# Two-layer decoder: moving the second group's cross-attention values and the next mapped keys from layer 1's token loop to the end of the experts

## The chip, the cores and the metric

The kernel runs on one core of one Trainium2 chip. The metric is device time in microseconds (us) of one execution; the median of several runs is compared. Engines are named as in the profile: PE is TensorE (PEld its weight loads), DVE is VectorE, ACT is ScalarE, POOL is GpSimd, and SP's queue issues most DMAs.

## The reference

Sixteen sequences of 256 tokens with 256 features go through two pre-norm decoder layers. Each layer adds three blocks to x. Layer 0: causal linear attention, cross-attention to a context of 77 rows for each sequence, and a mixture of 16 experts (top 2, limited capacity). Layer 1: self-attention with a low-rank latent for keys and values, cross-attention to the same context, and a quantized gated feed-forward block. What matters here is layer 1's cross-attention:

```python
def _L1_xattn_ref(Q, K, V, Wq, bq, Wk, bk, Wv, bv, Wo, bo, mask):   # K = V = ctx_1024
    q = Q @ Wq + bq
    k = K @ Wk + bk
    v = V @ Wv + bv
    scores = jnp.einsum('bqd,bkd->bqk', q, k) * scale
    scores = jnp.where(mask == 0, jnp.asarray(-1000000000.0, scores.dtype), scores)
    probs = jax.nn.softmax(scores, axis=-1)
    attn = jnp.einsum('bqk,bkd->bqd', probs, v)
    return attn @ Wo + bo
```

Neither k nor v depends on x: they can be formed whenever the context and the weights are there.

## The kernel before

**Tiling.** The 4096 tokens are 32 tiles of 128 rows, held on the chip as `E.xs[i]`; a group is four tiles, that is two sequences, so there are `NG = 8` groups. All arithmetic is in 32-bit floats.

**Stages.** `l0_attention` and `l0_cross` are layer 0's attentions; `l0_experts` goes over the 16 experts and writes their rows to device memory (`moe_y`); `l1_tokens` does everything of layer 1 up to the feed-forward block; `l1_ffn` is that block. `l0_experts` and `l1_tokens` are planned separately, but one program follows the other without a barrier, so work of `l1_tokens` that needs no expert starts on PE as soon as the last expert's products (`ps_y`, `ex_y`) are through.

**How `l1_tokens` begins.** Each token's row is x plus two expert rows. `l0_gather` fetches them with two indirect DMAs for a tile (`ex_yg`, issued on POOL, six buffers), `l0_add` adds them on DVE. `front_by_sequence(0)` does this for two tiles at a time: gathers, adds, `layernorm` (statistics and h on DVE, the two steps `ln_rstd` on POOL between them), transposes (`ps_ht`, `hT`), and the projections to the latent and the queries (`ps_pr`). `scores(0)`, the second half, and `front_by_sequence(1)` come next.

**The loop.** For each group g the loop runs over its four tiles: `weighted(i)` finishes tile i's self-attention (`ps_pt` transposes, `ps_av`, `ps_po`), `scores(i + 1)` begins the next one's (`ps_sc`, maxima `sa_top` on DVE, exponentials on ACT, `sa_e` scaled on POOL). Generators are stepped in between: `front(g + 2)`, `combine(g + 2)` (gathers and adds), `cross(g - 1)` (cross-attention of the group before) and `vals`, the values of the group after.

**Keys and values of the cross-attention.** The query, key and output weights are folded beforehand (`X.wqk`, `X.wb`, `X.wvo`). `keys_of(b0)` makes the mapped keys of four sequences, that is two groups: two tiles `ps_k` and one `ps_kb` on PE, each evacuated by ACT to `cx_k0`, `cx_k1` and `cx_kb`. `values(g)` makes what one group needs: `ps_v` on PE (one tile, four products), `cx_v` on DVE, and `cx_bias` in two steps on POOL. Before an even group, `values` first calls `keys_of`. All these tiles have two buffers. Group 0's are recorded ahead of the loop; the others' in the last tile of each turn of the loop.

**What sets the order.** The code above only records operations. `Plan.issue` then simulates the engines with fixed costs and puts the operations in order of their planned begin; on the chip each engine takes its operations in that order. A rank decides among those that could begin within 150 ns of the earliest on an engine: the number of the operation in the recording, plus 60 for those recorded under `urgent(-60)`, the lowest first. A buffer ring adds two rules (`slot_time`): a tile begins only once the tile recorded before it in its ring has begun, and only when the buffer's old user is done. The ring `pp` holds nearly all of PE's outputs in four PSUM buffers, so their order is that of the recording:

```python
    if tile.prior and not tile.prior.started and tile.prior.name not in op.tiles:
        return None
    if tile.older is not None:
        if tile.older.users:
            return None
```

All planned instructions are issued from one helper, so the profile gives L363 for nearly every row; the tiles' names tell them apart.

## Time and profile before

| what | value |
|---|---|
| median of 3 runs | 1718.7 us (1716.73 to 1720.42) |
| profiled execution, its own time | 1710.65 us |
| its span, first to last instruction | 1708.9 us |
| mean granted TensorE clock | 0.963 |
| PE / DVE / ACT / POOL busy | 92% / 65% / 45% / 27% |
| last expert's products (`ps_y`) end | 912.6 us |
| first gather for layer 1 issued | 915.67 us |
| first transpose of layer 1 (`ps_ht`) | 926.58 us |
| last gather issued | 1065.3 us |

Times in a row of the timeline are: start from the beginning of the span, duration, engine, line, operation, output<-inputs, shape, count, and in brackets the engine's idle time before it and what ended it. A busy PE is not PE at its peak. The granted clock is the share of full speed that the throttle allows TensorE.

### The profile page before, as it was taken

Reading aid. Unit: us, or ns where it says so; the run is one execution under the profiler, and the core shown is the slowest. Engines: PE = TensorE matmul, PEld = TensorE weight load, DVE = VectorE, ACT = ScalarE, POOL = GpSimd, SP = SyncE. Lnnn points to the kernel's source line nnn. Section 1 sums busy time; section 2 is a strip of 40 time slices with the busy share of each in tenths; the row PEclk is TensorE's granted clock in tenths of the full one; section 3 lists DMA queues with packets and bytes.
Section 4 is the critical chain, followed back from the end, with each engine's and each line's share of the span. In section 5 each row is a group of like instructions: output and inputs, shape, how many; then the busy total and the mean of one; then the engine's idle time right before and its main releaser. Section 6 shows DMA issues by size and latency. Waiting matters only on the chain.

```text
span 1708.9 us, 24351 instructions
## 1 busy us (share of the span) xinstructions
PE 1564.8 (92%) x9076; PEld 1040.7 (61%) x9076; DVE 1117.3 (65%) x2214; ACT 763.5 (45%) x1965; POOL 458.1 (27%) x538
## 2 busy tenths in 40 slices
PE   6999997998996799999997999999999699999799
PEld 3666664665664577777775665666666444433387
DVE  7988885999996343211223779866767543899951
ACT  4333324667765211211112555555555353667850
POOL 5332112355455200000004787433343200000000
PEclk9999998999997699999998999999999899999899
DMA  6000005611111153433331121000000000001111
GB/s 188 1 1 1 2 3 148 188 47 37 33 40 41 60 163 129 134 131 122 113 99 56 44 65 50 1 1 1 0 1 1 1 1 0 25 25 62 38 49 49
DMA packets 95783, 92.01 MB, mean 54 GB/s; under 512 B 32486, under 2 KB 85438, under 8 KB 95666
## 3 DMA queue, kind: packets, MB, share of 16 engines
q1 hardware_dynamic: 89522, 73.91, 13.8%
q0 software_dynamic: 6144, 16.57, 3.1%
q8 instruction: 71, 1.16, 0.3%
q14 instruction: 46, 0.38, 0.1%
HBM read 52.70 MB, written 36.70 MB: 52 GB/s over the span
## 4 chain that ended last, share of the span: by engine, by line
PE 55%; DVE 27%; issue 7%; ACT 5%; POOL 2%; DMA 2%; SPq 1%; POOLq 0%; DVEq 0%; ACTq 0%
PE ps_y L363 7%; PE ps_h L363 7%; PE ps_pr L363 6%; PE ps_av L363 5%; PE ps_gate L486 5%; PE ps_out L486 5%; PE ps_sc L363 4%; PE ps_pt L363 3%; PE ps_v L363 2%; DVE x L363 2%; DVE sa_top L363 2%; PE ps_po L363 2%; DVE lx_mx L363 2%; DVE lx_s L363 2%; DVE ff_g L1995 2%
## 5 line engine op out<-in xcount | busy, mean ns | idle before, releaser
L363 DVE COPY ex_y<-ps_y 128x256 f32<-128x256 f32 x80 | 33.6, 423 | 217.1 <-PE ps_y L363 217.1
L363 POOL DMA_INDIRECT ex_yg<-moe_y,slot x64 | 63.1, 986 | 344.0 <-DMA moe_y<-ex_y 326.8
L486 PE MATMUL ps_up<-ff_x,ffn_up 128*128 128x512 f32 x336 | 147.0, 595 | 7.1 <-DVE ff_pu L1866 4.3
L363 POOL TENSOR_TENSOR sa_e<-sa_e,sa_rec 128x1024 f32<-128x1024 f32 x64 | 121.4, 1905 | 118.8 <-PE ps_pt L363 64.2
L363 ACT ACTIVATE sa_e<-ps_sc,sa_top 128x256 f32<-128x256 f32 x256 | 118.0, 484 | 74.6 <-DVE sa_top L363 72.3
L363 PE MATMUL ps_h<-ex_xT,w 128*128 128x320 f32 x512 | 144.6, 440 | 0.5 <-ACT ex_h L363 0.5
L363 PE MATMUL ps_y<-w,ex_h 128*128 128x256 f32 x640 | 141.0, 379 | 1.6 <-DVE ex_y L363 1.6
L363 PEld LDWEIGHTS ps_y<-w,ex_h 128*128 128x128 f32 x640 | 121.6, 190 | 20.1 <-DVE ex_y L363 2.0
L363 ACT ACTIVATE ex_h<-ps_h 128x640 f32<-128x640 f32 x64 | 44.9, 703 | 186.6 <-PE ps_h L363 186.6
L363 PEld LDWEIGHTS ps_h<-ex_xT,w 128*128 128x128 f32 x512 | 97.2, 193 | 40.9 <-issue 1.8
L486 PEld LDWEIGHTS ps_up<-ff_x,ffn_up 128*128 128x128 f32 x336 | 63.0, 190 | 91.0 <-issue 73.2
L486 PE MATMUL ps_out<-ffn_down,ff_g 128*128 128x256 f32 x384 | 84.9, 385 | 11.6 <-issue 11.6
L363 ACT ACTIVATE lx_s<-lx_s,lx_mx 128x77 f32<-128x77 f32 x256 | 87.9, 346 | 16.3 <-DVE lx_mx L363 15.9
L486 PE MATMUL ps_gate<-ff_x,ffn_gate 128*128 128x512 f32 x192 | 85.3, 608 | 6.4 <-DVE ff_x L1968 6.4
L486 PEld LDWEIGHTS ps_out<-ffn_down,ff_g 128*128 128x128 f32 x384 | 74.2, 194 | 22.7 <-issue 12.4
L363 DVE TENSOR_REDUCE sa_top<-ps_sc 128x4 f32<-128x1024 f32 x64 | 76.3, 1214 | 14.9 <-PE ps_sc L363 14.6
L363 DVE TENSOR_TENSOR la_at<-ps_sc,la_tri 128x1024 f32<-128x1024 f32 x64 | 75.8, 1213 | 8.6 <-PE ps_sc L363 8.6
L363 POOL DMA_INDIRECT moe_x<-rh,slot x64 | 64.0, 999 | 43.7 <-issue 12.4
L363 PE MATMUL ps_sc<-sa_latT,sa_q 64*128 64x256 f32 x512 | 69.1, 396 | 2.8 <-ACT sa_e L363 2.8
L363 PE MATMUL ps_pt<-ident,sa_e 128*128 128x128 f32 x512 | 65.2, 277 | 6.1 <-ACT ff_x L363 1.9
L486 PEld LDWEIGHTS ps_gate<-ff_x,ffn_gate 128*128 128x128 f32 x192 | 37.4, 195 | 53.9 <-issue 53.1
L363 PEld LDWEIGHTS ps_pt<-ident,sa_e 128*128 128x128 f32 x512 | 57.7, 142 | 15.1 <-issue 3.2
(297 smaller groups left out, 3429.5 us busy)
## 6 DMA issues: line engine op xcount, KB each, us to landing
w<-in_L_ffn_w SPq DMA_DIRECT2D x32, 512.0 KB
moe_x<-rt_zero SPq DMA_DIRECT2D x16, 640.0 KB
ex_xg<-moe_x SPq DMA_DIRECT2D x15, 640.0 KB
moe_y<-ex_y SPq DMA_DIRECT2D x15, 640.0 KB
x<-in_x SPq DMA_DIRECT2D x32, 128.0 KB
out_x<-x SPq DMA_DIRECT2D x32, 128.0 KB
ff_u<-ff_c SPq DMA_DIRECT2D x6, 512.0 KB
ff_c<-ff_u SPq DMA_DIRECT2D x6, 512.0 KB
```

What stands on the lines that cost most here:

```text
L363: made = getattr(getattr(self.nc, self.engine), self.method)(*self.args, **self.kwargs)
L486: E.nc.tensor.matmul(ps, a, b, start=n == 0, stop=n == last)
L1995: nc.vector.scalar_tensor_tensor(gp, low16(gq, I16), sg16, low16(sig, U16), ALU.mult, ALU.mult)
```

## The change

Three things change, all in `l1_tokens`. The mapped keys are kept in a dictionary by pair of groups, so that two pairs can be held. Ahead of the first group's front, under the same `urgent(-60)`, the program now also records the second group's values and the mapped keys of the third and fourth groups. And the loop's first turn forms no values; `values(2)` in the second turn finds its keys made, and from then on the loop is as it was. The operations, their sizes and the numbers of buffers stay the same.

```diff
-        keys = SimpleNamespace()
+        keys = {}
 
         def keys_of(b0):
 
             cols = slice(b0 * S2, b0 * S2 + GK)
-            keys.mapped = []
+            mapped = []
 ...
-                keys.mapped.append(t)
+                mapped.append(t)
 ...
-            keys.term = t
+            keys[b0 // 4] = mapped, t
 
         def values(g):
 
-            if g % 2 == 0:
+            if g // 2 not in keys:
                 keys_of(2 * g)
                 yield
+            mapped, term = keys[g // 2]
             b0 = 2 * (g % 2)
-            C = SimpleNamespace(kT=[t[:, b0 * S2 : (b0 + 2) * S2] for t in keys.mapped])
+            C = SimpleNamespace(kT=[t[:, b0 * S2 : (b0 + 2) * S2] for t in mapped])
 ...
-                bias, keys.term[:, b0 : b0 + 2, :].unsqueeze(2).to_broadcast([P, 2, 2, S2]),
+                bias, term[:, b0 : b0 + 2, :].unsqueeze(2).to_broadcast([P, 2, 2, S2]),
 ...
         with nc.urgent(-60):
+
             step(values(0), 2)
+            step(values(1))
+            keys_of(4)
         f = front_by_sequence(0)
 ...
-            vals = values(g + 1) if g + 1 < NG else none
+            vals = values(g + 1) if 0 < g < NG - 1 else none
```

## The prediction

> **What bounds the kernel now.** I read the page first, for the engines and the chain; then the stretches, cut at the places where the moved work stands; then the timeline round the end of the experts; last the chain through the first turns of the token loop.

> ```profile
> PE 1564.8 (92%) x9076; PEld 1040.7 (61%) x9076; DVE 1117.3 (65%) x2214; ACT 763.5 (45%) x1965; POOL 458.1 (27%) x538
> ...
> PE 55%; DVE 27%; issue 7%; ACT 5%; POOL 2%; DMA 2%; SPq 1%; POOLq 0%; DVEq 0%; ACTq 0%
> ```

> TensorE is the bound over the span, but VectorE holds 27% of the chain, so a TensorE microsecond is worth a microsecond only in some stages. The stretches (columns: length, then busy time and count of PE, PEld, DVE, ACT, POOL; granted clock; DMA) say which:

> ```profile
> core 0: us, PE busy (x) PEld busy (x) DVE busy (x) ACT busy (x) POOL busy (x), PEclk, DMA share, GB/s
> ...
> 918.20:926.58 8.38, 0.00 (x0) 0.03 (x1) 5.83 (x12) 0.00 (x0) 6.07 (x8) 0.64 0.28 78
> 926.58:930.84 4.26, 4.01 (x11) 3.06 (x12) 2.55 (x6) 0.74 (x2) 3.72 (x4) 0.50 0.22 64
> ...
> 957.00:986.60 29.60, 28.57 (x157) 19.69 (x158) 22.08 (x43) 20.26 (x68) 24.05 (x22) 0.94 0.20 58
> 986.60:1043.80 57.20, 53.02 (x298) 34.81 (x297) 48.95 (x101) 29.21 (x98) 44.25 (x39) 1.00 0.19 56
> ...
> 1090.50:1146.70 56.20, 55.15 (x315) 36.42 (x314) 43.54 (x94) 31.98 (x112) 22.44 (x17) 1.00 0.00 1
> ...
> 1017.00:1067.00 50.00, 46.77 (x259) 30.61 (x257) 45.31 (x93) 25.21 (x87) 37.70 (x36) 1.00 0.20 57
> ```

> From 918.20 to 926.58 PE does nothing and ACT does nothing: everybody waits for the first gathered rows. From 1090 on PE is 98% busy. Between them, where the gathers still run on POOL, PE has some slack (53.02 of 57.20) and DVE is nearly full (45.31 of 50, 91%).

> ```profile
> 916.31 1.89 PE L363 MATMUL ps_v<-cx_wvo,w_ctx_T 128*77 128x256 f32 x8
> ...
> 919.52 0.95 POOL L363 DMA_INDIRECT ex_yg<-moe_y,slot  x1 [0.31 <-issue]
> ...
> 922.32 1.80 DVE L363 SCALAR_TENSOR_TENSOR x<-ex_yg,wgt,x 128x256 f32<-128x256 f32 x1 [0.31 <-DMA ex_yg<-moe_y,slot]
> 923.00 0.83 POOL L363 TENSOR_TENSOR cx_bias<-cx_kb,cx_on 128x308 f32<-128x308 f32 x1
> ...
> 924.88 0.34 POOL L363 TENSOR_TENSOR ln_rstd<-ln_mv,eps 128x2 f32<-128x2 f32 x1 [1.05 <-DVE ln_mv L363]
> ...
> 926.58 1.09 PE L363 MATMUL ps_ht<-ident,h 128*128 128x128 f32 x4 [8.38 <-issue]
> ...
> 986.82 1.89 PE L363 MATMUL ps_v<-cx_wvo,w_ctx_T 128*77 128x256 f32 x8
> ...
> 1042.48 1.53 PE L363 MATMUL ps_pt<-ident,sa_e 128*128 128x128 f32 x12 [1.09 <-ACT cx_k L363]
> ```

> This is the path to the first transpose: gather 4, its add, the statistics, two POOL steps (ln_rstd), h, transpose. The second group's values stand at 986.82; the mapped keys of groups three and four end at 1038, and their evacuation on ACT holds PE up at 1042.48.

> ```profile
> 982.14 2.95 DMA ex_yg<-moe_y,slot
> ...
> 999.28 1.53 PE ps_pt L363 x12
> ...
> 1020.83 2.35 DVE sa_top L363 x2
> ```

> The chain is not on PE where the moved work stands: from 974 to 999 it runs through POOL, gathers and DVE adds, and from 1020.8 through DVE.

> **The change part by part.**

> *Removed from the loop, PE.* values(1): 8 matmuls, 1.73 us in the chain's row at 916.47. keys_of(4): 8 matmuls ps_k, 2.34 us, and 4 ps_kb, 1.04 us. Together 5.11 us, the most that the loop can give.

> *Added before the first group, PE.* The same 5.11 us, started at 918.20: values to 919.93, ps_k to 922.27, ps_kb to 923.31. The tiles of this PSUM ring are taken in the order of the program, four buffers: the fourth new tile, ps_kb, needs the buffer of the first ps_v, which cx_v frees at 921.62, before its turn. The first transpose needs the buffer of the second ps_v, freed by the second cx_v on DVE, which stands ahead of h on the same engine. So it fits, 3 us ahead of 926.58. Cost nothing; the cover is the wait for gathers, and without it the 5.11 us would be paid back whole.

> *ACT.* Three evacuations of 0.52 to 0.57 us go into a time in which ACT is idle until 927.49: nothing.

> *DVE.* One cx_v of 0.65 us moves ahead of the fourth add. The fourth gather has landed at 922.3; DVE by then has the third add and cx_v to do. Counted below.

> *POOL.* Two cx_bias steps move from 965 to the front, and more: ranks decide POOL's order. The sixteen new operations ahead of the group's gathers raise the rank of gathers 5 to 8 from 72-75 to 88-91, while the first cx_bias keep 74 and 75 and the new ones have 81 and 82. So all four come right behind gather 4 (ended 920.47), at 0.85 from start to start (965.24 to 966.09), till about 924.0; gather 5 (0.95 and 0.3 of issue) follows, and ln_rstd, waiting for the fourth add, comes behind it at about 925.5 in place of 924.88. Queued behind are gathers 6 to 8. Start of h: 0.6 us later. Bounds: 0, if ln_rstd is planned ahead of gather 5, and +1.9 (0.6 and one more gather of 1.27). I take 0.6. Gathers 6 to 8 come 0.5 to 3 us later; the second half's h was ready at 934.32 and done at 937.44, after the first scores' maxima, which covers that.

> *The adds against POOL.* An add of 0.48 us took 1.80 at 922.32 and ended 0.29 after cx_bias. At 1043.41 six adds beside sa_e and two cx_bias took 1.23, 1.03 and 0.89 for the first three: one add got through between two POOL steps. By that the fourth add ends near 924, as before; that is in the 0.6.

> [...]

> *Clock.* After the empty 8.38 us PE ran at half clock for 4.26 us, with 4.01 busy: 2.0 us lost. The gap left is 3.3 + 0.6 = 3.9 us. The stretch from 957 has a granted clock of 0.94, 3.4 us of half clock, behind an idle time of only 1.75 and 0.35 us at 954.35 to 957.14. So 3.9 us will bring the half clock again: 0, bounds -2.0 (no half clock) and +1.7 (half of another 3.4 us).

> *What the loop makes of the 5.11 us.* From 986.60 to 1043.80 DVE is busy 48.95; without the cx_v of 0.65 it is 48.30. The fullest stretch shown ran DVE at 45.31 / 50 = 0.906; at that rate 48.30 takes 53.3 us, 3.9 less than 57.20. PE would need 47.6 of it. So 3.9 of 5.11 stay and 1.2 go to waits for DVE. Bounds 0 (DVE, POOL and gathers keep their pace) and 5.11; I take 3.9, since the later stretches show that the loop goes at PE's pace when DVE has room. Behind it PE is the bound and hands the gain on to the end. The two adds beside cx_bias at 964.78 and 966.34 took 1.53 and 0.90 in place of 0.47 and 0.45; with cx_bias gone DVE wins 1.5 there, and PE idles 1.03 in that stretch: 0.4 taken, bounds 0 and 1.0.

> Sum: -3.9 - 0.4 + 0.6 + 0 = -3.7 us. The profiled execution took 1710.65 (span 1708.9), so 1706.95 for one like it; the median of the runs is 8.05 higher, 1718.7, and the forecast for it is 1715.0.

> **The rivals.**

> *Nothing comes of it.* The chain says that at 986 and 1035 PE was not what ended last; if the gathers, POOL's sa_e and DVE's order stay the pace to 1066, PE only idles more (0.63 us of wait for DVE at 1066.49 becomes 5 or so). Then -0.4 + 0.6: 1718.9, give or take 2. For it: the chain, POOL's load of 44.25 in 57.20. Against: PE was 53.02 of 57.20 busy, so some of its work did hold the others up, the 1.09 us behind cx_k's evacuation among it.

> *Slower: POOL's order at the front.* If ln_rstd falls behind the four cx_bias and two gathers, h comes 1.9 later, PE's gap grows to 5.2 and one more half-clock window costs 1.7; if then the loop, whose gathers all come 1.6 later up to 965, keeps nothing, the time is 1718.7 + 1.9 + 1.7 = 1722.3. It decides from a first transpose after 928.5. For it: four POOL steps stand where one stood. Against: ln_rstd has a rank of 44 and yields only to what starts before it is ready; POOL's work up to 965 is only 1.64 us more.

> *It all counts.* The moved work fits and the half clock goes too: -5.1 - 1.0 - 2.0 + 0.6 = -7.5, 1711.2. The row at 957 speaks against it.

> **How the numbers follow.** A measurement of this kernel can tell about 0.2%, 3.4 us, from no change. The forecast case (1712 to 1717, chance 0.56, most of it beyond 3.4) and the full gain (0.08) give faster 0.50 and 0.14 to same; nothing (0.20) gives 0.17 to same and 0.03 to slower; POOL's order (0.16) goes to slower but for 0.01. So faster 0.50, same 0.32, slower 0.18. The range goes from the full gain, 1711.2, to the slower case's near side, 1721.8; what it leaves out is about 0.15.

> **What would show it.** Right: no ps_k and no ps_v at the places of 986 and 1035; PE busy about 5 of the 8.4 us behind 918; first transpose at about 927.2; four cx_bias in a row behind the fourth gather; the steps of the later turns (102.8 us for two groups) as before, but earlier by 3 to 4 us. Wrong, if the keys of groups five and six (before at 1144.71) come less than 1 us earlier: then DVE or POOL set the pace; if the first transpose is later than 928.5; or if the planner's order of the loop's first two groups differs so that PE idles more than 10 us between 927 and 1067 (now 11.2, summed from its gaps in the timeline).

## The result, and the profile after

The changed kernel is slower, by a little: its median is 1720.65 us (20 runs, 1717.18 to 1726.34), that of before on the same chip 1717.44 us (20 runs), a ratio of 1.0022 with a 95% interval of [1.0013, 1.0031], or 3.8 us. The forecast was 3.7 us the other way.

Two profiles are compared here by the time behind the end of the last expert product (912.58 us in before, 916.77 in the changed kernel; that difference of 4.19 us lies ahead of the change). The profiled execution of the changed kernel took 1721.74 us, its span 1720.0. The page's engines and chain:

```profile
PE 1573.7 (91%) x9076; PEld 1044.3 (61%) x9076; DVE 1122.2 (65%) x2216; ACT 763.1 (44%) x1963; POOL 459.0 (27%) x538
...
PE 54%; DVE 28%; issue 7%; ACT 5%; POOL 2%; DMA 2%; SPq 1%; POOLq 0%; DVEq 0%; ACTq 0%
```

DVE has two instructions more (2216 for 2214) and ACT two fewer: the planner gave it two more evacuations. The page tells little else, so I go to the front of the layer, in the timeline:

```profile
920.51 3.62 PE L363 MATMUL ps_v<-cx_wvo,w_ctx_T 128*77 128x256 f32 x16
...
923.96 2.24 PE L363 MATMUL ps_k<-w_ctx_T,cx_wqk 128*128 128x308 f32 x8
924.03 1.78 DVE L363 SCALAR_TENSOR_TENSOR x<-ex_yg,wgt,x 128x256 f32<-128x256 f32 x1 [0.86 <-DMA ex_yg<-moe_y,slot]
924.70 0.82 POOL L363 TENSOR_TENSOR cx_bias<-cx_kb,cx_on 128x308 f32<-128x308 f32 x1
...
927.17 1.30 PE L363 MATMUL ps_kb<-w_ctx_T,cx_wb 128*128 128x308 f32 x4 [0.98 <-DVE cx_v L363]
927.25 0.91 POOL L363 TENSOR_TENSOR cx_bias<-cx_bias,cx_drop 128x308 f32<-128x308 f32 x1
...
928.31 1.06 POOL L363 DMA_INDIRECT ex_yg<-moe_y,slot  x1 [0.15 <-issue]
...
929.38 0.20 POOL L363 TENSOR_TENSOR ln_rstd<-ln_mv,eps 128x2 f32<-128x2 f32 x1
...
930.95 0.71 PE L363 MATMUL ps_ht<-ident,h 128*128 128x128 f32 x4 [2.47 <-issue]
```

The front is what the prediction drew: all the moved products before the first transpose, POOL's four `cx_bias` in a row (the first and the last are shown), then a gather, then `ln_rstd`. The first transpose comes 14.17 us behind the last expert product, in before 14.00. Nothing is lost here yet. Next the stretches, from 14.5 us behind the last expert product, cut where tiles 3, 7, 8, 10 and 13 finish their self-attention (the start of the adds `x<-x,ps_po`); columns as before. First the kernel before, then the changed one:

```profile
927.08:998.82 71.74, 64.23 (x355) 45.78 (x353) 54.64 (x104) 43.02 (x142) 56.59 (x51) 0.95 0.18 52
998.82:1050.75 51.93, 48.86 (x263) 31.31 (x264) 45.83 (x97) 25.51 (x87) 39.13 (x36) 1.00 0.18 51
1050.75:1062.15 11.40, 11.40 (x61) 6.87 (x61) 9.03 (x18) 5.88 (x15) 9.61 (x10) 1.00 0.23 65
1062.15:1089.07 26.92, 26.29 (x148) 17.25 (x148) 23.53 (x51) 13.28 (x48) 13.62 (x12) 1.00 0.08 23
1089.07:1125.11 36.04, 35.11 (x208) 22.87 (x206) 25.55 (x49) 20.50 (x71) 13.74 (x10) 1.00 0.00 1
```

```profile
931.27:1003.44 72.17, 63.49 (x347) 45.42 (x346) 53.98 (x104) 43.29 (x142) 55.97 (x49) 0.93 0.18 54
1003.44:1055.14 51.70, 47.98 (x255) 29.79 (x256) 44.83 (x92) 23.08 (x82) 33.98 (x32) 0.97 0.15 44
1055.14:1068.68 13.54, 12.32 (x65) 7.15 (x65) 13.26 (x23) 7.82 (x24) 9.53 (x9) 1.00 0.11 31
1068.68:1100.04 31.36, 28.68 (x154) 18.71 (x153) 25.42 (x53) 11.23 (x40) 18.29 (x17) 0.95 0.14 42
1100.04:1135.96 35.92, 33.47 (x194) 21.51 (x192) 26.14 (x51) 20.43 (x71) 13.74 (x10) 1.00 0.00 1
```

PE's idle time (length less busy) is 12.14 us in before and 18.75 in the changed kernel. Up to tile 3 (71.74 and 72.17 us) and from there to tile 7 (51.93 and 51.70 us) the two need about the same time, though `values(1)` is gone from the first of these stretches and `keys_of(4)` from the second: what left PE didn't shorten them. Then tiles 7 to 10 take 44.90 us for 38.32, with more DVE and POOL work in them than before. From tile 10 on nothing more is lost (the changed kernel is 6.8 us behind at tile 10, 6.7 at tile 13 and 4.8 at tile 31). The chain of waits in the changed kernel's stretch of tiles 8 to 10:

```profile
1071.19 0.95 POOL ex_yg L363
1072.15 0.30 issue
1072.45 2.76 DMA ex_yg<-moe_y,slot
...
1075.30 2.83 DVE x L363
...
1080.16 0.61 DVE sa_aT L363
1080.77 0.04 issue
1080.81 2.62 PE ps_po L363 x8
```

PE stands from 1078.61 to 1080.81 because `sa_aT` is on DVE, behind adds that waited for gathers. In the kernel before, the same view suggests why the moved work was worth so little where it stood (the experiments e7 and e15 test it). `values(1)` stood at 986.82, where the chain runs through POOL, gathers and DVE (974 to 999, shown ahead). `keys_of(4)` stood at 1034.92 to 1038.30, and there the chain is on DVE from 1020.83 until POOL takes it over at 1048.65:

```profile
1026.10 4.13 DVE x L363 x4
...
1034.94 0.18 DVE ln_mv L363
...
1048.65 1.89 POOL sa_e L363
```

In before the last gather is issued 152.70 us behind the last expert product, here 168.06.

### The profile page after: what moved, and what is told of

Its sections match the earlier page's. It is cut to its first block, busy times and chain, and to the rows that moved or that the text cites. A ratio compares the mean times of both kernels' runs of the same rounds, so it can differ in the third digit from the quotient of the medians.

```text
span 1720.0 us, 24344 instructions
## 1 busy us (share of the span) xinstructions
PE 1573.7 (91%) x9076; PEld 1044.3 (61%) x9076; DVE 1122.2 (65%) x2216; ACT 763.1 (44%) x1963; POOL 459.0 (27%) x538
## 4 chain that ended last, share of the span: by engine, by line
PE 54%; DVE 28%; issue 7%; ACT 5%; POOL 2%; DMA 2%; SPq 1%; POOLq 0%; DVEq 0%; ACTq 0%
PE ps_y L363 7%; PE ps_h L363 7%; PE ps_pr L363 6%; PE ps_av L363 5%; PE ps_gate L486 5%; PE ps_out L486 5%; PE ps_sc L363 4%; PE ps_pt L363 3%; DVE x L363 3%; PE ps_v L363 2%; PE ps_po L363 2%; DVE lx_mx L363 2%; DVE sa_top L363 2%; DVE lx_s L363 2%; DVE h L363 2%
## 5 line engine op out<-in xcount | busy, mean ns | idle before, releaser
L363 DVE COPY ex_y<-ps_y 128x256 f32<-128x256 f32 x80 | 33.7, 424 | 217.0 <-PE ps_y L363 217.0
L363 POOL DMA_INDIRECT ex_yg<-moe_y,slot x64 | 63.3, 989 | 348.8 <-DMA moe_y<-ex_y 327.7
L363 ACT ACTIVATE sa_e<-ps_sc,sa_top 128x256 f32<-128x256 f32 x256 | 118.2, 485 | 77.8 <-DVE sa_top L363 75.5
L363 POOL TENSOR_TENSOR sa_e<-sa_e,sa_rec 128x1024 f32<-128x1024 f32 x64 | 121.5, 1906 | 116.8 <-PE ps_pt L363 65.5
L363 PE MATMUL ps_h<-ex_xT,w 128*128 128x320 f32 x512 | 144.6, 440 | 0.5 <-ACT ex_h L363 0.5
L363 PE MATMUL ps_y<-w,ex_h 128*128 128x256 f32 x640 | 141.0, 379 | 1.4 <-DVE ex_y L363 1.4
L363 PEld LDWEIGHTS ps_y<-w,ex_h 128*128 128x128 f32 x640 | 121.5, 190 | 20.0 <-DVE ex_y L363 1.8
L363 ACT ACTIVATE ex_h<-ps_h 128x640 f32<-128x640 f32 x64 | 44.9, 704 | 186.5 <-PE ps_h L363 186.5
L363 PEld LDWEIGHTS ps_h<-ex_xT,w 128*128 128x128 f32 x512 | 97.2, 193 | 40.9 <-issue 1.8
L363 ACT ACTIVATE lx_s<-lx_s,lx_mx 128x77 f32<-128x77 f32 x256 | 87.9, 346 | 16.7 <-DVE lx_mx L363 16.4
L363 DVE TENSOR_REDUCE sa_top<-ps_sc 128x4 f32<-128x1024 f32 x64 | 76.4, 1215 | 19.1 <-PE ps_sc L363 18.8
L363 DVE TENSOR_TENSOR la_at<-ps_sc,la_tri 128x1024 f32<-128x1024 f32 x64 | 75.8, 1215 | 8.6 <-PE ps_sc L363 8.6
L363 POOL DMA_INDIRECT moe_x<-rh,slot x64 | 63.9, 999 | 43.2 <-issue 12.4
L363 PE MATMUL ps_pt<-ident,sa_e 128*128 128x128 f32 x512 | 64.5, 275 | 9.4 <-DVE cx_v L363 4.0
L363 PE MATMUL ps_sc<-sa_latT,sa_q 64*128 64x256 f32 x512 | 70.2, 401 | 0.8 <-ACT sa_e L363 0.8
L363 PE MATMUL ps_po<-sa_wvo,sa_aT 128*128 128x256 f32 x256 | 63.4, 391 | 7.4 <-ACT sa_aT L363 4.4
```

Of the source, the lines that this page charges most:

```text
L363: made = getattr(getattr(self.nc, self.engine), self.method)(*self.args, **self.kwargs)
```

## The experiments

Three theories. **Theory 1**: the first three turns go at the pace of the gathers, POOL and DVE, each working in a fixed order; PE's time is not what ends last, so taking work from it there wins nothing. **Theory 2**: the front costs it, POOL's extra `cx_bias` standing ahead of the gathers. **Theory 3**: the planner, whose costs for DVE and POOL are not the chip's (it counts 0.32 us for an add of gathered rows that took 0.45 to 2.94 in before, and 0.64 for a `cx_bias` step that took 0.75 to 1.00), makes a new order of the early turns, and any new order moves the time. Every ratio is against runs of before on the same chip in the same rounds; on some chips before itself takes 1750 us, most of the difference lying in the stages ahead of this one (e12's span is 24.8 us longer than that of the change's first profile, and its last expert product ends 22.7 us later).

| kernel | ratio to before | tile 13 | last gather | PE idle to tile 13 |
|---|---|---|---|---|
| before (first profile; c1; c3) | 1 | 212.5; 214.3; 214.7 | 152.7; 153.0; 153.9 | 12.1; 11.0; 12.5 |
| the change (first; c2; e12) | 1.0022; 1.0029; 1.0011 | 219.2; 217.9; 220.1 | 168.1; 168.3; 170.5 | 18.8; 20.8; 23.9 |
| e1 values alone | 1.0044 | 225.2 | 161.7 | 21.2 |
| e2 keys alone | 0.9989 | 220.6 | 171.0 | 18.6 |
| e5 front alone | 1.0005 | 215.1 | 156.3 | 12.6 |
| e6 bias late | 1.0014 | 213.9 | 170.9 | 19.0 |
| e7 order kept | 1.0021 | 226.0 | 161.5 | 19.6 |
| e8, e15 fewer products | 1.0000; 1.0005 | 219.0; 212.4 | 156.3; 151.7 | 16.8; 13.4 |
| e11 late gathers | 0.9968 | 216.9 | 169.5 | 13.3 |
| e4 before, gated | 0.9991 | 215.3 | 321.8 | 13.4 |
| change, gated (e3; e10) | 0.9929; 0.9933 | 209.5; 208.1 | 312.5; 311.8 | 12.1; 11.4 |
| e9 bias late, gated | 0.9968 | 204.7 | 314.2 | 9.3 |
| e13, e14 no gathers in the loop | 0.9936; 0.9889 | 207.3; 202.8 | (none) | 7.1; 8.5 |

The last three columns are of one profiled execution each, in us: tile 13 and the last gather by the time behind the last expert product, and PE's idle time from 14.5 us behind it to tile 13. Two profiles of one kernel differ by up to 2.2 us at tile 13 and by about 5 us in the idle time, so the ratios decide.

**Each part by itself (e1, e2).** e1 is the change without the line `keys_of(4)` at the front, e2 the change without `step(values(1))` there, and both do the rest in the loop.

> Only the second group's values go early (1.73 us of PE, one cx_v, two cx_bias); the mapped keys stay in the loop. Theory 1 (the first three turns of the loop, while the gathers run, are paced by DVE and POOL in order; PE work taken out there is not won, and the new order lets the gathers slip behind the turns' own work): the front costs 0.2 us, little PE work is taken out, the gathers end within 3 us of their old place (152.7 us behind the last expert product), and the time is within 2 us of before. Theory 2 (the front: cx_bias ahead of gathers 5 to 8): all of the added POOL and DVE work is here, so the time is like that of the whole change, +3.8 us or so.

Measured: 1.0044 [1.0029, 1.0059].

> Only the mapped keys of groups three and four go early (3.38 us of PE, three ACT evacuations, nothing on DVE or POOL); the second group's values stay in the loop. Theory 1: the gathers slip as in the whole change (they end some 10 to 15 us later than before), and the time is +2 to +5 us. Theory 2 (the front): POOL's front has two cx_bias as before, so the time is that of before or up to 3.4 us less.

Measured: 0.9989 [0.9972, 1.0007]. The smaller part costs 7.7 us and the larger nothing, and together they cost 3.8: the parts don't add up, which speaks for Theory 3, against any sum of parts. Theory 1 as it was put missed both (within 2 us for e1, 2 to 5 us slower for e2), and e1 is also beyond Theory 2's 3.8 us. In both, PE's idle time grew by more than the work that was taken out (to 21.2 us in e1 and 18.6 in e2, from 11 to 12.5).

**The front by itself (e5, e6).** e5 is before, with the same products, evacuations and POOL steps done once more at the front, into buffers that nobody reads:

```diff
+        def spare():
+            ...   # ps_v, cy_v, two cy_bias; two ps_k, ps_kb and their evacuations
         with nc.urgent(-60):
             step(values(0), 2)
+            spare()
```

> The kernel before, and at its front the moved work done once more into buffers that nobody reads (8 + 8 + 4 matmuls, three evacuations, one cx_v, two cx_bias), so that the front is that of the change and the loop's work that of before. Theory 1 (the loss is in the loop's first turns): +0.2 to +2 us. Theory 2 (the front): +3.8 us or more. Theory 3 (any new order of the early turns moves the time by some us, up or down, since the plan's costs for DVE and POOL are not the chip's): anywhere from -5 to +8, with the difference arising behind the third tile and not at the front.

Measured: 1.0005 [0.9993, 1.0016]. The front costs about 0.9 us (at most 2.7), which agrees with its term in the sum (0.6). Theory 2 doesn't explain the 3.8 us.

e6 is the change, but the second group's two `cx_bias` steps wait for the loop's first turn:

```diff
+            if g == 1:
+                yield
             bias = wk.tile([P, 2, 2, S2], F32, name="cx_bias", tag="cx_bias")
```

> The whole change, but the second group's two cx_bias stay in the first turn of the loop; POOL's front then has two cx_bias ahead of gathers 5 to 8 in place of four. Theory 1: the gathers end late as in the change, and the time is that of the change within 2 us. Theory 2 (the front): that of before or less, at least 3 us faster than the change. Theory 3: as likely up as down against the change.

Measured: 1.0014 [1.0001, 1.0027], against 1.0029 [1.0016, 1.0042] for the change in the same rounds (c2); the intervals overlap. Its profile has tile 3 4.4 us earlier than the profile of before on the same chip (c1), but tile 10 only 0.5 us: time won in the first turn is lost by the third. Here are the two controls of these rounds:

> The kernel before once more, for a profile on the chip of the other runs of this set. All theories: its token stage (last expert product to last tile's add, 436.0 us in the first profile) comes out within 3 us of that if the stage repeats itself; if it differs by 5 us or more, single profiles of this stage don't carry differences of a few us.

> The change once more, on the chip of the other runs of this set: 1.002 of before by the first measurement; its gathers end some 15 us later than before's in the same set if that is the order and not the chip.

c1's token stage took 437.7 us, 1.7 more than the first profile's; c2 gave 1.0029. From 14.5 us behind the last expert product to tile 13 c1 took 199.77 us with PE busy 188.75, c2 203.38 with 182.55. So PE had 6.2 us less to do (5.11 moved; c1 also had about 15 us of half clock there, c2 8.5) and idled 9.8 us longer: 3.6 us lost. This is the clearest account of the change.

Half clock doesn't explain the loss: the changed kernel's runs had the higher granted clock (a mean of 0.9635 in c2's 11 runs against 0.9617 in the 27 of before; 0.9580 against 0.9543 in the set of e12). And in the change's three profiles (first, c2, e12) half clock took 17.1, 8.5 and 3.4 us of this stretch, PE was busy 185.9, 182.6 and 181.7 us and idle 18.8, 20.8 and 23.9, and tile 13 came at 219.2, 217.9 and 220.1: PE time that the clock gave back became waiting too.

**What PE's time in the loop is worth (e8, e15).** Both are before with the order of every engine unchanged; only products of `values(1)` and `keys_of(4)` are cut down, while the planner still counts them in full:

```diff
+            E.nc.tensor.matmul(
+                ps[:, :4], a, b[:, :4], start=n == 0, stop=n == last, wide=free(ps))
```

> Before, with every engine's order as it was; only the products of values(1) and keys_of(4) in the loop have 4 columns in place of 256 or 308 (planned at their full cost, evacuated with one column repeated), so 5.11 us of TensorE's time in the loop become about 0.5; nothing is done at the front. Left out: the values of group 1 and the mapped keys of groups 2 and 3. This measures what 4.6 us of TensorE's work at these places are worth by themselves. Theory 1: 0 to 1.5 us, ratio 0.9991 to 1.0000, the idle time of TensorE between tile 3 and tile 10 grows by 3 us or more. Theory 3: 3.5 to 4.6 us, ratio 0.9973 to 0.9980, tile 10 at -3.5 to -4.6.

Measured: 1.0000 [0.9986, 1.0014]. In the trace `ps_v` took 0.65 us for 1.89, and `ps_k` with `ps_kb` 1.50 for 3.38: an instruction with 4 columns still takes time, and about 3.1 us had left PE, not 4.6. The interval allows a gain of 2.4 us, so the ratio says only that they didn't all count. Hence e15, which issues one product for each of the four tiles:

> As e8_few_columns, with every engine's order that of before, but of the products of values(1) and keys_of(4) only the first of each of the four tiles is issued, with 4 columns; e8 has shown that one such product still takes 0.13 us, two TensorE instructions each: about 1.0 us of the 5.11 stays, 4.1 leave. Left out: the values of group 1 and the mapped keys of groups 2 and 3. If TensorE's time at these places counts: 3 to 4.1 us, ratio 0.9976 to 0.9983. Theory 1 (VectorE, GpSimd and gathers pace the early turns): 0 to 1 us, ratio 0.9994 to 1.0000, and TensorE idles 3 us or more longer than in c3_before up to tile 13.

Measured: 1.0005 [0.9990, 1.0021].

```profile
1039.47 0.61 PE L368 MATMUL ps_k<-w_ctx_T,cx_wqk 128*128 128x4 f32 x4
1039.93 0.36 PE L368 MATMUL ps_kb<-w_ctx_T,cx_wb 128*128 128x4 f32 x2
```

`ps_k` and `ps_kb` now took 0.83 us for 3.38, `ps_v` 0.24 for 1.89, and 4 us less work on PE gave nothing; the interval allows 1.7 us at most. The traces show the order of every engine as it was in before. Two things make the zero less sharp. The granted clock was lower in these runs (a mean of 0.9587 against 0.9608), and in this set a clock lower by 0.001 goes with 1.3 us more (a line fitted to its runs); by that estimate e15 would be about 1.4 us faster at the clock of before. And the expected 3 us more of idle time didn't show in its one profile (13.4 against 12.5 in c3 and 11.0 in c1): against c1, whose execution had the same mean granted clock (0.958), PE was busy 4.2 us less and idle 2.3 us longer, and tile 13 came 1.8 us earlier, of which 0.1 was left at tile 31, behind 3.41 us more of half clock. So of the 4 us little or nothing counted, and not the 3 or more that PE's pace would have given.

> The kernel before, unchanged, for its profile on the same chip: 11 to 13 us of idle time of TensorE between the first transpose and tile 13, last gather at 152 to 157 us behind the last expert product, tile 13 at 212 to 218 us.

c3 had 12.5 us of idle time, the last gather at 153.9 us and tile 13 at 214.7.

**The order (e7, e11).** e7 is the change, planned as if the moved steps still stood at their old places: recorded there, counted in full, not issued. In the plan, and in the trace, the order of PE in the loop is then exactly that of before.

```diff
+            if self.ghost:
+                return
             made = getattr(getattr(self.nc, self.engine), self.method)(*self.args, **self.kwargs)
```

> The change, but the planner still counts the moved steps at their old places in the loop as well (planned there with their full costs, not issued), so that on TensorE the loop's other products stand in exactly the order of before. The planner's order at the front is the changed kernel's. Theory 1 (VectorE, GpSimd and the gathers pace the first three turns whatever the order on TensorE): the 5.11 us are not won, but the gathers do not slip either; tile 10's last add at +0 to +1.5 us against before, ratio 0.9995 to 1.0010. Theory 3 (it is the new order that the planner made of the freed time that eats the gain): with the old order the freed time is won, tile 10 at -2.5 to -4.5 us, ratio 0.9975 to 0.9985. If neither holds, it is as slow as the change, 1.0022 or more, with tile 10 at +5 or more. Last gather: 152 to 157 us behind the last expert product by both theories, 168 if neither.

Measured: 1.0021 [1.0009, 1.0033], as slow as the change; both theories were wrong about it. Keeping PE's order saves nothing. DVE's and POOL's orders still differ from before's, by the front; its last gather came at 161.5. By the traces, up to tile 31, e7 has on all four engines the order of e5, with the moved steps left out at their old places. So the two differ by that work alone, and taking it out gained nothing: 1.0021 for e7 against 1.0005 for e5, each against before on its own chip. This is the prediction's term itself, measured with every order kept, though on two chips.

e11 is before with the last eight tiles' gathers planned no earlier than in the change:

```diff
+                    with nc.after(LATE.get(tiles[n], 0)):
                         held[n] = l0_gather(E, back, routed, tiles[n])
```

> Before, with the gathers of the last eight tiles planned no earlier than the changed kernel plans them (5 to 11 us later); the order on TensorE and ScalarE is before's, on VectorE and GpSimd only these gathers and adds stand later. Theory 1, with the slip as the cause of the excess loss: tile 10's last add at +2.5 to +4.5 us against before, ratio 1.0015 to 1.0026. If the slip is only a symptom (the turns are slow for another reason and the gathers follow): -0.5 to +1 us, ratio 0.9997 to 1.0006. Theory 3 (any new order moves the time) allows both signs, 1 us or more.

Measured: 0.9968 [0.9954, 0.9982]: 4.5 us faster by the medians, where Theory 1 with the slip as the cause had it slower. The slip of the last gathers, which had looked like the cause, is none in before's order; by itself it helped, though its runs also had a higher granted clock than before's (0.9583 against 0.9543), and at tile 13 its profile is not ahead (216.9).

> The change itself once more, on the chip of the other three: 1.001 to 1.004 by the runs so far, tile 10 at +3.5 to +7 us.

e12 gave 1.0011 [0.9995, 1.0026].

**The gathers (e13, e14, e3, e4, e9, e10).** e13 and e14 are before and the change with `later = none`, so that the loop has no gathers and adds.

> Before without the gathers and adds of the loop. Left out: the expert rows of tiles 8 to 31. Theory 1: the early turns then go at TensorE's pace, the order of TensorE being nearly the same; tile 10 at -8 us or better against before, ratio below 0.996; TensorE idles under 8 us between the first transpose and tile 13 (11 to 12 in before). Theory 3 alone, with nothing held up by gathers: within 0.998 to 1.002.

> The change without the gathers and adds of the loop; left out as in e13_before_no_gathers, with which it is to be compared. Theory 1: with nothing else setting the pace the 5.11 us count, less about 0.9 at the front: 3.5 to 5 us faster than e13_before_no_gathers, the ratios 0.0020 to 0.0029 apart. Theory 3 or a cost of the change that has nothing to do with gathers: no faster than e13, or slower.

Measured: 0.9936 [0.9916, 0.9956] and 0.9889 [0.9870, 0.9908], the medians 1738.51 and 1731.45 us: without the gathers the change wins 7.1 us. That is more than the 3.5 to 5 expected; e14's runs had a higher granted clock (0.9590 against 0.9562), which by the spread of the runs in this set goes with about 1.9 us, and leaves about 5. In e13 tile 10 came 5.2 us earlier than in the first profile of before, where 8 had been expected. The stretch from tile 3 to tile 7, first e13, then e14:

```profile
1027.11:1076.93 49.82, 49.73 (x274) 32.31 (x273) 31.93 (x74) 26.86 (x90) 19.81 (x16) 1.00 0.00 1
```

```profile
1024.14:1071.27 47.13, 47.13 (x269) 30.84 (x268) 34.20 (x75) 23.14 (x79) 18.00 (x15) 1.00 0.00 1
```

PE has next to no idle time left here, and the work taken from it shortens the stretch. To tile 31 the profiles are 4.81 us apart, near the 5.11 that left the loop. The traces of e13 and e14 show the orders of PE and ACT of before and of the change (but for four transposes `ps_pt` that stand elsewhere in e14), so the same order on PE that loses with the gathers wins without them. So the moved work fits at the front, and its place in the loop is free of cost only because gathers, adds and what waits for them set the pace. This is the core of Theory 1, shown from both sides (e15, and e7 beside e5; e14 beside e13).

In e3 and e10 (the change) and e4 (before) the loop's gathers stay, spread over the turns by a planned earliest time:

```diff
+                    with nc.after(30000 + 49000 * (g - 2)):
                         held[n] = l0_gather(E, back, routed, tiles[n])
```

> The whole change, but a group's gathers may be planned no earlier than the turn of the loop that records them (every 49 us of the plan), so that they no longer crowd the first turns. Theory 1: DVE and POOL have room in the first turns, PE sets the pace there too, and the 5.1 us count: 4 to 10 us faster than the change, below before. Theory 2 (the front): the front is untouched, so the time stays that of the change within 2 us. A third possibility: the gathers become late for their own turns, and the time is over 5 us longer.

> The kernel before with the same bound on the gathers. Theory 1: the first turns lose their waits for DVE and gathers (PE idles 11 us between 927 and 1067 before): 2 to 7 us faster than before, and about 4 to 5 us slower than the change with the bound. Theory 2 (the front): no change, within 2 us of before.

> The same kernel as e3_after_gated, on the chip and in the rounds of the other three: by Theory 1 0.992 to 0.995 again, last gather past 290 us behind the last expert product, tile 10 at -3 us against before. If the first result was one chip's, it is within 0.998 to 1.002.

Measured: 0.9929 [0.9911, 0.9947] for e3, 0.9933 [0.9915, 0.9951] for e10, 0.9991 [0.9976, 1.0005] for e4. Spread out, the gathers hold the change up far less, and it is 12 us faster than before: the fastest kernel here that leaves nothing out. The stretch of e10 from tile 8 to 10:

```profile
1088.81:1114.47 25.66, 25.11 (x140) 16.49 (x142) 22.73 (x51) 11.32 (x40) 14.96 (x14) 1.00 0.14 39
```

25.66 us for tiles 8 to 10 stand against 31.36 in the change. Before gained little by the same gate (1.6 us, where Theory 1 had 2 to 7): in e4's one profile tile 13 is at 215.3, and behind it PE stood for 3.18 us at 1198.07 and tile 31 came at 446.6 (436.0 in before). A spread of the gathers alone is thus no sure gain. And behind the same gate the change is 10 to 11 us faster than before, twice the 5.11 us that left the loop: the PE work can account for half of that at most. No run explains the rest; the planner's new order (Theory 3) is the candidate left.

> The change with the gathers of the loop planned later (as in the kernel e3_after_gated) and with the second group's two cx_bias steps left in the loop's first turn (as in e6_bias_late). Theory 1: the gathers no longer stand between the early turns' steps on GpSimd and VectorE, so both gains add up: tile 3 at -5, tile 10 at -5 to -7 against before, ratio 0.990 to 0.993. Theory 3: the order is new once more, so anything between 0.993 and 1.001, with no reason to be better than e3_after_gated's 0.9929.

Measured: 0.9968 [0.9955, 0.9981]. Tile 13 is the earliest of all kernels that keep the gathers, at 204.7, 3.4 us ahead of e10; but tile 31 comes at 437.97, 5.5 us behind e10. The gains added up early, as Theory 1 said, and the later turns, planned anew, gave back more than these 3.4 us, as Theory 3 has it.

## Why the prediction was wrong, step by step

*The step that failed* is "what the loop makes of the 5.11 us". It divided DVE's busy time by 0.906, the rate of the fullest stretch shown, and so made 3.9 us of gain. It was mis-sized because a busy share is no capacity: at tiles 3 to 7 DVE's rate was 0.88 in before and still only 0.87 in the change, and what ended last where the moved work stood was not PE but gathers, adds and the steps queued behind them on DVE. The runs show about 0 in place of the 3.9: e15, with 4 us off PE and all orders as they were, gave 0 (1.7 at most; about 1.4 if the clock is allowed for), and e7 beside e5 gave nothing either. The chain of waits shown in the prediction already said so, running through POOL, gathers and DVE from 974 to 999 and through DVE from 1020.8; the rival "nothing comes of it" read it rightly and was given 0.20, though its time, 1718.9, was too low as well. (That PE would need 47.6 us should read 47.9 by the prediction's own 5.11; nothing rests on it.)

*The term that was missing* is DVE's own. The prediction let it fall by one `cx_v` of 0.65 us. Durations summed by tile names from 14.5 us behind the last expert product to tile 13:

| DVE, us | before (first, c1, c3) | the change (first, c2, e12) | e8 |
|---|---|---|---|
| all | 175.6, 176.1, 174.6 | 180.9, 181.3, 180.7 | 174.2 |
| `h`, 30 steps | 17.6, 17.6, 17.4 | 21.2, 21.1, 21.4 | 17.1 |
| adds of gathered rows | 46.3, 46.7, 45.3 | 48.0, 48.6, 47.7 | 45.1 |

So DVE grows by 5 to 6 us in place of falling. Where `h` takes longer is to be seen in the timeline of the changed kernel:

```profile
1058.23 3.79 POOL L363 TENSOR_TENSOR sa_e<-sa_e,sa_rec 128x1024 f32<-128x1024 f32 x2
...
1058.27 4.55 DVE L363 TENSOR_SCALAR h<-x,ln_mv,ln_rstd 128x256 f32<-128x256 f32 x4 [0.18 <-POOL ln_rstd L363]
```

Of these four `h` two took 1.98 and 1.99 us, each as long as the `sa_e` (1.88 and 1.94 us) that POOL had just begun; most of the kernel's `h` take 0.40 or 0.41. In before one of the four at this place took 1.99, beside a `sa_e` of 1.88; up to tile 13 three steps took about 1.98 us in before and five in the changed kernel. The two more `ps_pt` evacuations on DVE add 1.4 us. From the last expert product to tile 13, each of the 12 `h` and adds of gathered rows in before that took 1.4 us or more, and each of the 16 in the changed kernel, ran beside a `sa_e` or a `cx_bias` on POOL and ended 0.15 us (`h`) or 0.28 to 0.29 us (adds) behind the end of one; most adds take 0.45 to 0.49. That the POOL step holds up the DVE step is my reading of these rows; no run tests it by itself. The prediction weighed this for the adds at the front, and not for what the loop's new order brings beside each other.

That DVE's growth makes up the 2 to 3 us beyond "nothing" is argued, not shown: e1 lost 7.7 us with a DVE sum of 175.8, and e7 lost 3.7 with 167.9. What exactly eats the rest is open. It isn't PE's order (e7, e14), nor the clock, nor the front alone as far as e5 can tell, and the slip of the gathers did no harm in before's order (e11).

*The front:* start +0.6 was forecast, +0.2 seen in the profile and 0.9 [-1.2, 2.7] measured by e5: both agree with it, the second loosely, since e5's runs had a higher granted clock than before's (0.9633 against 0.9617), which by a line fitted to this set's runs goes with 1.5 us. The gap ahead of the first transpose was 2.47 us and not 3.9, since `ps_kb` waited 0.98 for `cx_v`, which the second add (1.78 beside `cx_bias`) had made late; it cost nothing. POOL's order was exactly as worked out. Clock 0: right at the front (one stretch of half clock, 3.41 us, where before had 10.24, 6.0 of it in the empty time). In the loop stretches of half clock came and went: the change's first profile had three there (6.83, 3.41 and 3.41 us), c2 one and e12 none, and all three were slower than before.

*The -0.4 for adds freed of `cx_bias`:* not seen; tile 3 came 0.4 us later, not earlier. e6, which leaves these two steps in the loop, has tile 3 4.4 us earlier than c1: by that profile the steps were better where they stood, though over the whole kernel e6 is not clearly faster than the change.

*The rivals:* the slower one gave 1722.3, and before's 1718.7 times 1.0022 is 1722.5; yet by its own condition, a first transpose later than 928.5 (15.9 us behind the last expert product), it isn't what happened, for that stood at 14.17. So the agreement of the time is luck. "It all counts" has its work count only once the gathers are gone (e14).

*The signs:* the prediction called itself wrong if the keys of groups five and six came less than 1 us earlier. They came 6.7 us later (234.38 us behind the last expert product, in the profile of before 227.73). That sign held. The one on PE's idle time could tell nothing as it stood: it asked for more than 10 us between 927 and 1067, and before itself had 11.2. In the 140 us behind the first transpose it grew to 13.6 us (15.7 in c2, 18.7 in e12).

## What to carry to other kernels

Before counting work taken off an engine as time, follow the chain of waits through the very stretch that it leaves: where the chain runs through gathers and a second engine's queue, the freed time can become idle time, and busy shares such as 92% or a "rate" of 0.9 don't tell how much. To price such work, keep every engine's order and take only the work away; then take the suspected pace-setter away and move the work again. And where a planner orders the program, a change to one engine's work is a change to all engines' order: look at what now runs beside what (here `h` beside `sa_e`), and spread the transfers before moving the work.

## What the runs showed of the hardware that was not expected

```profile
1042.09:1045.50 3.41, 1.64 (x13) 0.95 (x11) 3.38 (x11) 3.38 (x15) 1.08 (x1) 1.00 0.13 38
1045.50:1052.33 6.83, 5.99 (x20) 4.39 (x20) 6.11 (x10) 5.19 (x16) 5.50 (x5) 0.50 0.05 13
```

- The 48 gathers and adds of tiles 8 to 31 (0.95 and 0.30 us of POOL, 0.5 to 0.8 us of DVE each) cost 0.64% of the time (e13), and with a third of them planned 5 to 11 us later, the orders on PE and ACT unchanged, the time was 0.32% shorter (e11; part of that goes with the higher granted clock of its runs, 0.9583 against 0.9543).
